# A new written order of the neighbourhood layer's parts in a period, and of the recurrence's units between them

## The chip, the cores and the metric

The kernel runs on one core of one Trainium2 chip. The metric is the device time of one execution in microseconds; of the kernel before there are three timed runs. The profile is of one further execution.

## The reference

Input `x` is (4, 56, 56, 128): four images of 3136 tokens with 128 channels. Four layers follow one another, each with residual sums. The change concerns the first two:

```python
# layer 0: 7x7 neighbourhood attention with 4 heads, then an MLP (128 -> 512 -> 128)
x = x + proj(softmax(q . k over the 7x7 window + rpb) @ v)      # q, k, v from layernorm(x)
x = x + gelu(layernorm(x) @ w_fc1 + b_fc1) @ w_fc2 + b_fc2
# layer 1: group norm, then 16 steps of a gated complex recurrence per position and channel
x = x + recurrence(gn(x))
#   forget = sigmoid(x Wf + bf + 2); let_in = sigmoid(x Wi + bi); delta = softplus(x Wd + bd) * 0.1
#   h <- forget * (A h) + delta * let_in * (B x), with A and B from 7x7 kernels by a Fourier transform
```

Layers 2 and 3 are softmax attention, mixtures of experts, a distance attention and expert choice. They come later in the program and their code is the same in both kernels.

## The kernel before

`neighbourhood_of_safe_scores` (L471) works layer 0 off in 28 stripes: 4 images times 7 stripes of 8 image rows, 448 tokens each. A stripe passes through 25 parts, small functions that each issue a few instructions: two of attention scores (`scores`, `more_scores`: TensorE at L653, the exponential on ScalarE at L662), the position bias (`bands`, `more_bands`: VectorE, L669), the sums over neighbours and their denominators (`start_sums`, `sums`, `more_sums`: TensorE, L683 to L711), `quotient` (VectorE, L719 and L720), `project` and `add_attention` (L725 to L737), `second_norm` (VectorE, L739: statistics, then an inverse root of twelve small steps that ends with `off`, L546), `norm_mlp` and `mlp_tokens`, `mlp_hidden` (TensorE L754, GELU on ScalarE L759), `mlp_out` (L768) and `add_mlp` (L778). `norm_ahead`, `tokens`, `keys` and `queries` prepare a stripe three ahead (L583 to L618), `values` makes v (L635 and L639), `statistics` takes the first norm's statistics of stripes further on, up to three of them a period, until all are taken.

The parts are written out in the table `PERIOD` as (name, lag): in period i the part works on stripe i + lag. The loop of L867 runs i from -1 to 29. Everything in it stands in a manual schedule (L827): TensorE, VectorE and ScalarE issue their instructions in exactly this written order, each in its own queue, and wait for one another by semaphores only. So the table's order is the order of each of the three queues.

Between the parts lies the recurrence of image 0, at places which three more tables give as (period after the start, position in the period, name): a piece at position p is issued just ahead of the p-th part.

```python
for i in range(-1, n + 2):
    for at, (name, lag) in enumerate(PERIOD):
        run_all(plan.get((i, at), ()))
        if 0 <= i + lag < n:
            parts[name](i + lag)
    run_all(plan.get((i, len(PERIOD)), ()))
```

`WAVES_AT` places the eight transform steps that make A and B (L1033 to L1072), one starting in each of the periods 1 to 8. `BEGIN` places the group norm of image 0 from period 8 on: `tokens` (28 transposes and seven ScalarE sums, L1095), `mean`, `squares` (seven ScalarE passes, L1112), `root`, `normalise`. `WORK` places the pieces of each of seven units (a quarter of the rows of `parts`, L1128), the first from period 10 and one every two periods. A unit has three gates on TensorE and ScalarE (`delta`, `forget`, `let_in`: L1159 and L1164), copies (`turned`, L1181), a logarithm (L1188), and some forty VectorE instructions over 224 or 448 columns (L1185 to L1282). Even periods from 10 to 24 are called even below; in the kernel before, most of a unit's VectorE work lies in an even period.

[...] Scores and the MLP's hidden sums share one buffer of four banks, the sums have two, and all else on TensorE shares a pool of two banks (`ps1`): `mlp_out`, `values` (two tiles), both token transposes, `keys`, `queries`, `project`, the gates, the transform's products and `turned_back`. A tile that takes one of these banks waits for the reader of an earlier tile.

ScalarE's functions need tables. `exp_table` and `gelu_table` (L825) call the function on one column, so that the table is loaded there. The functions of the recurrence (sigmoid, logarithm, square root) load others.

Of the kernel before, what the change touches and what calls it, by code (L numbers as in the profile page):

```python
# [38 lines left out]
NQ = EC // ET  # L39

PERIOD = (
    ("mlp_out", -2),
    ("exp_table", 1),
    ("norm_mlp", -1),
    ("more_sums", 0),
    ("norm_ahead", 3),
    ("scores", 1),
    ("add_mlp", -2),
    ("values", 1),
    ("more_scores", 1),  # L50
    ("tokens", 3),
    ("mlp_tokens", -1),
    ("quotient", 0),
    ("keys", 3),
    ("bands", 1),
    ("constants", 1),
    ("queries", 3),
    ("project", 0),
    ("start_sums", 1),
    ("more_bands", 1),  # L60
    ("add_attention", 0),
    ("mlp_hidden", -1),
    ("gelu_table", -1),
    ("second_norm", 0),
    ("sums", 1),
    ("statistics", 1),
)

WORK = (
    (0, 20, "delta"),  # L70
    (0, 23, "turned"),
    (1, 12, "softplus"),
    (1, 12, "sources"),
    (1, 14, "logarithm"),
    (1, 18, "let_in"),
    (1, 19, "forget"),
    (1, 21, "softplus_sum"),
    (1, 22, "source"),
    (1, 24, "source_gate"),
    (2, 4, "traces"),  # L80
    (2, 4, "fourths"),
    (2, 5, "fourths_trace"),
    (2, 7, "sums"),
    (2, 7, "sums_of_fourths"),
    (2, 11, "product_of_sums"),
    (2, 14, "pair"),
    (2, 18, "steps"),
    (2, 20, "result"),
    (2, 21, "result_sum"),
    (3, 1, "turned_back"),  # L90
    (3, 2, "added"),
    (4, 25, "statistics"),
)

BEGIN = (
    (0, 25, "tokens"),
    (1, 11, "mean"),
    (1, 14, "squares"),
    (1, 22, "root"),
    (2, 12, "normalise"),  # L100
)

WAVES_AT = (
    (0, 11, "products"),
    (1, 17, "squared"),
    (1, 17, "magnitudes"),
    (2, 10, "scaled"),
)
UNITS = 9
KK = 128  # L110
# [360 lines left out]
def neighbourhood_of_safe_scores(env: Env, f, work):  # L471
# [17 lines left out]
    with ExitStack() as ctx:  # L489
# [337 lines left out]
        with tc.manual_schedule(  # L827
# [39 lines left out]
# [7 lines that stand above are left out]
# [1839 lines left out]
def run_all(pieces):  # L2713
    for piece in pieces:
        piece()
# [201 lines left out]
```

## Time and profile before

| | |
|---|---|
| median of three runs | 2683.82 us (2681.54 to 2685.61) |
| the profiled execution's own time | 2683.05 us |
| its span, first to last instruction | 2681.3 us |
| TensorE, VectorE, ScalarE busy | 2484.3, 2025.0, 1688.4 us |
| start of the first scores (L653) / end of the last `add_mlp` (L778), where the next layer begins | 32.85 us / 690.9 us |

The stage that the tables order is thus the stretch from 32.85 to 690.9 us, a quarter of the span. A busy TensorE is not TensorE at its peak, since the ends of matmuls are modelled. Idle time is listed before an instruction, with what ended it; on an engine that doesn't set the pace it costs nothing.

### The profile page before, as it was taken

What the parts mean: (1) busy time and instruction counts of PE and PEld (TensorE: products, weight loads), DVE (VectorE), ACT (ScalarE), POOL (GpSimd) and SP (SyncE); (2) the same over time, 40 slices, a digit from 0 to 9 for tenths busy, and PEclk for the clock granted to TensorE, in tenths of its full rate; (3) what the DMA queues carried; (4) which work ended last, traced back from release to release, by engine and by line L of the source; (5) the groups of instructions that cost most, each with busy time, mean ns of one, the idle gap of its engine ahead of it and who ended that gap; (6) DMA issues with size and microseconds to landing.
All of it is one profiled execution on the core that took longest, in us unless ns stands there. A gap on an engine that the chain in (4) does not pass through costs nothing.

```text
span 2681.3 us, 40144 instructions
## 1 busy us (share of the span) xinstructions
PE 2484.3 (93%) x14849; PEld 1338.1 (50%) x14849; DVE 2025.0 (76%) x5777; ACT 1688.4 (63%) x3539; POOL 4.4 (0%) x34
## 2 busy tenths in 40 slices
PE   5998898889999999999999999999999998997795
PEld 4676666667544544444454444444444443442333
DVE  6877999998488785879958877863788676766564
ACT  3789777775578774767733366565555565753671
POOL 0000000000000000000000000000000000000000
PEclk8999999999999999999999999999999998997687
DMA  5000000000000000000000000000000000001265
GB/s 134 10 10 2 2 2 2 2 1 2 9 1 1 1 0 1 1 1 1 0 11 0 1 1 1 1 1 1 1 1 1 0 1 1 1 1 75 98 251 180
DMA packets 39924, 54.01 MB, mean 20 GB/s; under 512 B 4105, under 2 KB 35444, under 8 KB 35621
## 3 DMA queue, kind: packets, MB, share of 16 engines
q1 hardware_dynamic: 39716, 51.34, 6.0%
q8 instruction: 119, 1.95, 0.3%
q14 instruction: 89, 0.72, 0.1%
HBM read 44.78 MB, written 6.42 MB: 19 GB/s over the span
## 4 chain that ended last, share of the span: by engine, by line


## 5 line engine op out<-in xcount | busy, mean ns | idle before, releaser
L1969 PE MATMUL s_ps<-zT,xnT 128*128 128x448 f32 (+1 forms) x1400 | 652.9, 557 | 11.6 <-ACT e L1976 11.2
L2052 PE MATMUL o_ps<-e,keep 128*128 128x448 f32 (+1 forms) x1376 | 645.6, 553 | 0.0
L1976 ACT ACTIVATE e<-s_ps 128x448 f32<-128x448 f32 x688 | 363.9, 542 | 444.3 <-PE s_ps L1969 436.4
L1969 PEld LDWEIGHTS s_ps<-zT,xnT 128*128 128x128 f32 (+1 forms) x1400 | 238.1, 189 | 232.4 <-issue 181.5
L2052 PEld LDWEIGHTS o_ps<-e,keep 128*128 128x128 f32 (+1 forms) x1376 | 242.0, 190 | 218.1 <-issue 216.9
L1783 ACT ACTIVATE d_ps<-d_ps,half 112x448 f32<-112x448 f32 x412 | 249.2, 606 | 157.5 <-PE d_ps L1772 156.3
L1777 DVE TENSOR_REDUCE found<-d_ps 112x1 f32<-112x448 f32 x372 | 224.3, 618 | 74.5 <-PE d_ps L1772 71.1
L1513 PE MATMUL y_ps<-experts,xnT 128*112 128x512 f32 x448 | 217.8, 608 | 3.4 <-ACT d_ps L1783 2.4
L1518 DVE TENSOR_TENSOR gated<-y_ps,gate 112x512 f32<-112x512 f32 x224 | 151.6, 687 | 47.2 <-PE y_ps L1513 45.1
L1772 PE MATMUL d_ps<-q_near,k_near 32*112 32x448 bf16 x784 | 154.6, 410 | 14.9 <-ACT d_ps L1783 7.7
L1523 DVE TENSOR_TENSOR gated<-gated 112x512 f32<-112x512 f32 (+1 forms) x336 | 152.7, 462 | 3.3
L202 PE MATMUL xT_ps<-ident,xn 112*128 112x112 f32 x672 | 112.4, 280 | 28.6 <-ACT xn L1613 18.6
L1772 PEld LDWEIGHTS <-k_near 32*112 32x112 bf16 x784 | 47.0, 126 | 178.6 <-issue 166.7
L202 PEld LDWEIGHTS xT_ps<-ident,xn 112*128 112x128 f32 x672 | 79.1, 145 | 99.1 <-ACT xn L1613 54.5
L1513 PEld LDWEIGHTS y_ps<-experts,xnT 128*112 128x112 f32 x448 | 75.8, 179 | 99.8 <-issue 60.1
L768 PE MATMUL f_ps<-w_fc,h 128*112 128x128 f32 x896 | 113.1, 282 | 4.7 <-ACT h L759 3.9
L1613 ACT ACTIVATE xn<-x,g_off,g_rs 112x128 f32<-112x128 f32 x224 | 94.5, 484 | 26.2 <-DVE g_off L1603 9.7
L768 PEld LDWEIGHTS f_ps<-w_fc,h 128*112 128x112 f32 x896 | 102.8, 179 | 15.5 <-ACT h L759 10.0
L583 ACT ACTIVATE xn<-x,off,rs 112x128 f32<-112x128 f32 x224 | 89.3, 480 | 30.3 <-DVE off L546 30.3
L669 DVE TENSOR_TENSOR e<-e,band 112x1792 f32<-112x1792 f32 (+3 forms) x56 | 98.9, 1783 | 4.4 <-ACT e L662 4.4
L754 PE MATMUL h_ps<-zT,w_fc 128*128 128x448 f32 x224 | 101.4, 600 | 0.6 <-ACT zT L748 0.6
L1164 ACT ACTIVATE parts<-g_ps,gates_b 128x224 f32<-128x224 f32 x168 | 65.6, 445 | 57.6 <-PE g_ps L1159 45.0
(387 smaller groups left out, 4057.9 us busy)
## 6 DMA issues: line engine op xcount, KB each, us to landing
lot<-in_L_ffn_lots SPq DMA_DIRECT2D x32, 1024.0 KB
out_x<-x SPq DMA_DIRECT2D x28, 224.0 KB
x<-in_x SPq DMA_DIRECT2D x3, 1568.0 KB
x<-in_x SPq DMA_DIRECT2D x7, 224.0 KB
parts<-in_waves SPq DMA_DIRECT2D x8, 173.0 KB
out<-found SPq DMA_DIRECT2D x64, 2.0 KB
w_fc<-in_L_conv_w_fc SPq DMA_DIRECT2D x2, 256.0 KB
experts<-in_L_ffn_expert_w SPq DMA_DIRECT2D x1, 512.0 KB
```

Source lines behind the costliest of these rows:

```text
L202: self.nc.tensor.transpose(ps[:, j * P : (j + 1) * P], xn[:, j, :], self.ident[:P, :P])
L754: nc.tensor.matmul(h_ps[:, k, :GW], w_fc1[:, k * 128 : (k + 1) * 128], held[i]["zT"], start=True, stop=True,)
L768: nc.tensor.matmul(f_ps[:, j, :], h[:, k, j * P : (j + 1) * P], w_fc2[:, k, :], start=(k == 0), stop=(k == 3),)
L1513: nc.tensor.matmul(y_ps, held["xnT"][g][:, j * P : (j + 1) * P], self.experts[:, 4 * i : 4 * i + 4, :], start=True, stop=True,)
L1518: nc.vector.tensor_tensor(gated[:, some, :], y_ps, gate[:, some].unsqueeze(2).to_broadcast([P, 4, C]), ALU.mult,)
L1523: nc.vector.tensor_tensor(gated[:, :n, :], gated[:, :n, :], gated[:, n : 2 * n, :], ALU.add)
L1772: nc.tensor.matmul(d, held["k"][part, h, :], held["q"][g][part, :], start=True, stop=True)
L1777: nc.vector.tensor_reduce(self.found[:, self.most : self.most + 1], d, AX.X, ALU.max)
L1783: nc.scalar.activation(d, d, AF.Relu, bias=self.half, accum_out=self.found[:, self.sums : self.sums + 1],)
L1969: nc.tensor.matmul(s_ps[i * n : (i + 1) * n, :GW], self.xnT[:, at : at + n], zT, start=True, stop=True,)
L1976: nc.scalar.activation(e[:n], s_ps[:n, :GW], AF.Exp)
L2052: nc.tensor.matmul(sums[:, :GW], self.keep[:n, k, :], e[:n], start=(k == 0 and g - 1 not in pairs), stop=last,)
```

## The change

Four tables get other contents. No part, no instruction and no size is changed. In `PERIOD` all 25 entries stand as before with the same lags, in another order: `more_sums` comes ahead of `mlp_out`; `mlp_tokens` ahead of the scores; `statistics` moves from the end to behind `more_scores`; `add_mlp` moves behind `values` and `statistics`; `project` and `start_sums` move ahead of `keys`, and `queries` to the end; `sums` moves ahead of `add_attention`; `gelu_table` moves ahead of `mlp_hidden`; `more_bands` moves behind `sums`.

The units begin three positions later (`delta` at position 23). `softplus_sum`, `source` and `source_gate` move from the end of the odd period to the start of the even one, the gates `let_in` and `forget` to position 22, behind the GELU. `sums_of_fourths` to `steps` stand together at position 13, ahead of `bands`. The group norm's `mean` and `squares` move to the start of period 9, and `normalise` to position 22 of period 10.

```diff
 PERIOD = (
+    ("more_sums", 0),
+    ("norm_mlp", -1),
+    ("exp_table", 1),
     ("mlp_out", -2),
-    ("exp_table", 1),
-    ("norm_mlp", -1),
-    ("more_sums", 0),
     ("norm_ahead", 3),
+    ("mlp_tokens", -1),
     ("scores", 1),
-    ("add_mlp", -2),
     ("values", 1),
     ("more_scores", 1),
+    ("statistics", 1),
+    ("add_mlp", -2),
     ("tokens", 3),
-    ("mlp_tokens", -1),
     ("quotient", 0),
-    ("keys", 3),
+    ("constants", 1),
     ("bands", 1),
-    ("constants", 1),
-    ("queries", 3),
+    ("gelu_table", -1),
     ("project", 0),
     ("start_sums", 1),
+    ("keys", 3),
+    ("mlp_hidden", -1),
+    ("sums", 1),
+    ("add_attention", 0),
+    ("queries", 3),
     ("more_bands", 1),
-    ("add_attention", 0),
-    ("mlp_hidden", -1),
-    ("gelu_table", -1),
     ("second_norm", 0),
-    ("sums", 1),
-    ("statistics", 1),
 )
 
 WORK = (
-    (0, 20, "delta"),
     (0, 23, "turned"),
-    (1, 12, "softplus"),
-    (1, 12, "sources"),
-    (1, 14, "logarithm"),
-    (1, 18, "let_in"),
-    (1, 19, "forget"),
-    (1, 21, "softplus_sum"),
-    (1, 22, "source"),
-    (1, 24, "source_gate"),
-    (2, 4, "traces"),
-    (2, 4, "fourths"),
-    (2, 5, "fourths_trace"),
-    (2, 7, "sums"),
-    (2, 7, "sums_of_fourths"),
-    (2, 11, "product_of_sums"),
-    (2, 14, "pair"),
-    (2, 18, "steps"),
-    (2, 20, "result"),
-    (2, 21, "result_sum"),
-    (3, 1, "turned_back"),
-    (3, 2, "added"),
+    (0, 23, "delta"),
+    (1, 4, "softplus"),
+    (1, 13, "logarithm"),
+    (1, 14, "sources"),
+    (1, 22, "let_in"),
+    (1, 22, "forget"),
+    (2, 1, "softplus_sum"),
+    (2, 2, "source"),
+    (2, 2, "source_gate"),
+    (2, 7, "traces"),
+    (2, 7, "fourths"),
+    (2, 8, "fourths_trace"),
+    (2, 10, "sums"),
+    (2, 13, "sums_of_fourths"),
+    (2, 13, "product_of_sums"),
+    (2, 13, "pair"),
+    (2, 13, "steps"),
+    (2, 21, "result"),
+    (2, 22, "result_sum"),
+    (3, 3, "turned_back"),
+    (3, 8, "added"),
     (4, 25, "statistics"),
 )
 
 BEGIN = (
-    (0, 25, "tokens"),
-    (1, 11, "mean"),
-    (1, 14, "squares"),
-    (1, 22, "root"),
-    (2, 12, "normalise"),
+    (0, 23, "tokens"),
+    (1, 0, "mean"),
+    (1, 5, "squares"),
+    (2, 2, "root"),
+    (2, 22, "normalise"),
 )
 
 WAVES_AT = (
-    (0, 11, "products"),
-    (1, 17, "squared"),
-    (1, 17, "magnitudes"),
-    (2, 10, "scaled"),
+    (0, 9, "products"),
+    (1, 12, "squared"),
+    (1, 12, "magnitudes"),
+    (2, 1, "scaled"),
 )
```

## The prediction

> **What bounds the kernel now.** I read the page first, then busy time by stages, then the timeline and the table of waits inside the stages. The page says only that TensorE is busiest overall:
>
> ```profile
> span 2681.3 us, 40144 instructions
> PE 2484.3 (93%) x14849; PEld 1338.1 (50%) x14849; DVE 2025.0 (76%) x5777; ACT 1688.4 (63%) x3539; POOL 4.4 (0%) x34
> ```
>
> The four tables order only 32.85 to 690.9 us, so I cut that stretch where its limits change (the columns are us, then busy time of PE, PEld, DVE, ACT, POOL, then the granted clock):
>
> ```profile
> 32.85:95.99 63.14, 52.84 (x679) 40.24 (x679) 51.26 (x195) 33.13 (x62) 0.00 (x0) 0.81 0.29 62
> 95.99:221.62 125.63, 119.69 (x1598) 90.79 (x1594) 102.25 (x270) 113.42 (x194) 0.00 (x0) 1.00 0.03 9
> 221.62:310.51 88.89, 78.48 (x964) 58.79 (x964) 71.23 (x188) 76.68 (x140) 0.00 (x0) 0.98 0.01 2
> 359.36:409.10 49.74, 45.22 (x558) 33.66 (x557) 46.95 (x118) 36.98 (x65) 0.00 (x0) 0.90 0.01 2
> 554.22:601.70 47.48, 42.07 (x540) 31.09 (x536) 44.04 (x102) 36.73 (x65) 0.00 (x0) 0.96 0.01 2
> 630.33:690.90 60.57, 53.88 (x634) 40.48 (x632) 39.23 (x111) 29.00 (x52) 0.48 (x9) 0.97 0.00 1
> ```
>
> Row 2 is six periods of pure PE work: 95% busy. Rows 4 and 5 are two pairs of periods with a recurrence unit in each: DVE 94%, and the rest is mostly the step from one instruction to the next. So there are five pieces: a head, a PE-bound piece, the group norm's start, the DVE-bound units (310.51 to 630.33), a tail. In the PE-bound piece the timeline shows one real gap per period, and in the units the other things that matter, a wait for `quotient` and half-speed matmuls after it (L683 takes 1.86 us instead of 1.02):
>
> ```profile
> 183.10 0.98 PE L202 MATMUL xT_ps<-ident,xn 112*128 112x112 f32 x8
> 184.99 1.55 PE L1043 MATMUL f_ps<-parts,taps 113*64 113x196 f32 x16 [0.91 <-ACT xnT L599]
> 189.39 1.02 PE L683 MATMUL d_ps<-outside,pad_w 49*128 49x448 f32 x2
> ...
> 326.96 1.17 PE L730 MATMUL y_ps<-w_proj,oT 128*112 128x128 f32 x8 [2.42 <-DVE oT L720]
> 328.05 1.86 PE L683 MATMUL d_ps<-outside,pad_w 49*128 49x448 f32 x2
> ```
>
> [...] The trace shows such stretches in multiples of 3.41 us, but in the units after gaps of 2.3 to 2.5 us already (four of the five PE waits of that size), so I use the trace. [...]
>
> **The change, part by part.** Durations are steps from one start to the next in the timeline. No instruction and no DMA is added. The only DMAs in moved parts are the eight of `in_waves`; SP keeps their order, and their buffers come free earlier. Nothing is queued on POOL. Table loads: four per period in the PE-bound piece (exp, square root, sigmoid, GELU) and six per pair of unit periods, both before and after: `delta` behind the GELU loads exp itself, and the next `exp_table` then finds it there.
>
> *Head.* `statistics` now stands ahead of the first `bands` and the late constants on DVE. It fills DVE waits of 4.37, 2.88 and 0.37 us, but three stripes (4.17 us each) hold `bands` from 36.8 to 48.7 us, and `sums` on PE with it. The second scores then start at 56.6 instead of 52.4 us. DVE owes less afterwards (7.4 us); by the fourth scores I get 95.5 instead of 95.99. Gain 0.5.
>
> *PE-bound periods.* PE's parts add up to 19.75 us (20.4 with an edge stripe). The gap of 0.91 between `tokens` and what follows goes: `project` and `start_sums` (2.2 us) now cover ScalarE's copy. In its place `tokens` waits 0.32 us for a `ps1` bank, since the transform's copies come behind the second exponential (1.2 us). With 0.07 at `more_scores` that makes 20.2 instead of 20.73; ScalarE (18.9) and DVE (18.2 to 20.0) fit below. Six periods: gain 3.0.
>
> *Group norm's start.* `tokens` costs ScalarE 4.8 us, `squares` 5.4. New: `squares` stands ahead of the copy of zT and the exponential in period 9, so PE waits 3 us for a bank and runs at half speed for about 6.8 us (3 us lost). `delta` of unit 0 waits for `normalise` and `queries`, and DVE idles 4.4 us before `softplus`. Adding up from the scores of period 8 to the end of `second_norm` of period 11: 85.7 us against 88.9 (where DVE waited 7.8 us for `mlp_out` and 4.3 for `mean`). But then 1.8 us of DVE work (`softplus_sum`, `source`) that was done by then is still to do. Gain 1.4.
>
> *Units.* DVE's work per pair: twice 12.3 (`second_norm` 4.2, `quotient` 3.5, bands 3.4, two sums 1.2) and 21.2 for the unit, 45.9; with `statistics` (1.6 a period, until period 17) 49.0. Measured pairs were 48.9, 49.7, 51.9 (an inverse root of 2.65 in it), 45.9, 47.4, 47.5: waits of 4.6 us in six and a half pairs. That is all the units can give. In the new order DVE has 30.5 us of work in an even period and 15.4 in an odd one (each plus 1.6), so in the odd ones a chain must keep up. From the end of `second_norm` (off, L546): norms 0.15 to 3.45 (eight of 0.385 and steps between), copy of zT to 3.9, exponential to 5.6, `more_scores` 6.45, `tokens` 6.95, `project` behind `quotient` to 8.75, `start_sums` 9.8, `keys` 10.65, `mlp_hidden` 13.85, four GELUs 16.1, table 17.4, `let_in` 18.2. DVE needs it for `source_gate` after 0.78 + 0.54 + 0.65 + 1.6 + 0.6 + 3.5 + 1.1 + 1.9 + 0.6 + 1.5 + 4.2 + 1.9 = 18.9: margin 0.7. Without `statistics` it needs it at 17.3 and has it at 17.5: wait 0.2 to 0.35, and 0.65 more before an edge stripe. Ahead of the chain, `turned` and `delta` (with a table load, 5.4 us behind `result_sum`) end 0.3 us before `second_norm` does. In even periods PE waits 2.4 us at `values` (`add_mlp` now lies behind 7.9 us of unit work and `statistics`), 1.4 at `project` and up to 2.0 for `more_bands`; the first two cost nothing while DVE is busy, the last stands at the head of the chain: if PE is then at half speed, `mlp_out` ends 2.4 us later. I take 0.2 us a pair for four pairs, 1.7 for the last three together, and 0.7 for half speed: 3.2 in place of 4.6. Gain 1.4.
>
> *Tail.* Without units, `mlp_out` behind `more_sums` and ahead of `add_mlp`, then `quotient`, delays `quotient` by 0.9 us in period 26, of which 0.8 reaches the end. Loss 0.8.
>
> Sum: 0.5 + 3.0 + 1.4 + 1.4 - 0.8 = 5.5 us. The profiled execution took 2683.05 us, 1.75 more than its span, and 0.8 less than the median; its span would become 2675.8, and the median 2683.8 - 5.5 = 2678.3. What follows at 690.9 us is unchanged.
>
> Bounds of what the trace doesn't show: the head -2 to +7 (DVE's whole idle time), half-speed stretches in the start 0 to 3 us (shown by L683's 1.86 against 1.02), and in the units 0 to 2 us a pair.
>
> **Rivals.** *Larger gain.* The head keeps its 7.2 us of filled DVE idle time, because PE's later start is made up by fewer waits in the next two periods, and the odd chain never holds DVE: 7.2 + 3.0 + 1.4 + 4.6 - 0.8 = 15.4 at most, about 11 if half of the head's gain is eaten: 2673. For it: DVE has no gap from 45 to 95 us. Against it: PE has to restart at 56.6 us at half speed.
>
> *Slower.* The odd chain decides. If every wait for `more_bands` is followed by a half-speed stretch (four of five long waits were), the chain starts 2.4 us late, and DVE waits 1.7 us where the margin is 0.7 and about 2.5 where it is none: with the edge 0.65, 4 x 1.7 + 3 x 2.5 + 0.65 = 15. The other terms give 0.5 + 3.0 + 1.4 + 4.6 - 0.8 = 8.7, so the change loses from 8.7 / 7 = 1.2 us a pair on; at 15 it loses 6: 2690. Against it: in the even periods the earlier waits take the half-speed stretch first, where it is hidden, and then PE comes late enough to have less than 1 us left to wait.
>
> *No change.* DVE's work is fixed and bounds 310 to 630 us, and the start of the units is delayed by as much as PE gained before: 2683.
>
> **How the numbers follow.** Within 0.2% (5.4 us) is about what a measurement of this kernel can't tell from no change. Forecast 0.48 (own range 2673 to 2683; 0.30 of it faster, 0.18 same), larger gain 0.22, no change 0.10, slower 0.20. Faster: 0.30 + 0.22 = 0.52; same 0.18 + 0.10 = 0.28; slower 0.20. The range runs from the larger gain, with the head's bound partly taken, to the slower case: 2669 to 2690.
>
> **What would show it.** Right: periods of 20.2 us at full clock in the PE-bound piece, with no wait on xnT L599; `bands` at about 48.7 us; pairs of 46 to 49 us in the units, DVE idle before `source_gate` (L1198) below 1 us; `values` waiting for add_mlp in even periods. Wrong: DVE idle of over 1.2 us a pair before L1198, L778 or L1185 in the units; half-speed `mlp_out` at the head of odd periods; a PE-bound period still at 20.7; a tail more than 2 us longer; or any change behind the stage's end.

## The result and the profile after

The change makes the kernel slightly faster: the median goes from 2682.26 us (ten runs, 2679.13 to 2687.31) to 2673.87 us (ten runs, 2668.07 to 2679.25), a ratio of 0.9964 with a 95% interval of 0.9954 to 0.9975. 2678.3 had been forecast, in a range of 2669 to 2690. The profiled execution of the changed kernel took 2678.24 us against 2683.05, so it is one of its slower ones; the last section comes back to that spread.

The page of the changed kernel, its lines for the span and the busy time: the engines have the same work, and the span is 4.9 us shorter.

```profile
span 2676.4 us, 40173 instructions
PE 2478.0 (93%) x14849; PEld 1336.8 (50%) x14849; DVE 2024.6 (76%) x5777; ACT 1690.3 (63%) x3539; POOL 4.3 (0%) x34
```

Busy time by stages, cut at the same events as before (us, then busy PE, PEld, DVE, ACT, POOL, granted clock): the head, the six PE-bound periods, the group norm's start, two pairs of unit periods, the tail.

```profile
32.71:94.51 61.80, 51.11 (x684) 37.31 (x684) 56.10 (x223) 33.44 (x62) 0.00 (x0) 0.83 0.31 67
94.51:215.00 120.49, 118.19 (x1596) 90.01 (x1595) 100.82 (x253) 112.80 (x193) 0.00 (x0) 1.00 0.03 9
215.00:298.41 83.41, 77.24 (x979) 59.28 (x980) 66.65 (x181) 74.36 (x137) 0.00 (x0) 0.96 0.01 2
349.43:398.60 49.17, 42.06 (x542) 32.03 (x538) 46.92 (x117) 37.82 (x65) 0.00 (x0) 0.97 0.01 2
544.45:591.36 46.91, 41.18 (x534) 31.78 (x530) 44.06 (x102) 37.19 (x65) 0.00 (x0) 0.96 0.01 2
621.93:685.86 63.93, 56.63 (x609) 43.10 (x607) 39.05 (x111) 31.07 (x54) 0.48 (x9) 0.93 0.00 1
```

Against the rows of before, the head is 1.3 us shorter, the PE-bound piece 5.1, the start 5.5. In the PE-bound piece TensorE's idle time fell from 5.94 us (125.63 - 119.69) to 2.30, and its busy time by 1.5. The units as a whole (298.41 to 621.93) are 3.7 us longer, the tail 3.4 longer: 4.9 us are left. What follows took 1990.3 us before and 1990.6 after, to the end of the span.

The timeline of TensorE in one PE-bound period of the changed kernel shows what the gap became: the transform's matmuls (L1043) now come first, `tokens` waits 0.31 us for a bank, and `keys` (L605) finds its operand ready.

```profile
137.88 1.55 PE L1043 MATMUL f_ps<-parts,taps 113*64 113x196 f32 x16
139.74 0.60 PE L202 MATMUL xT_ps<-ident,xn 112*128 112x112 f32 x4 [0.31 <-ACT fa L1047]
140.18 0.38 PE L725 MATMUL y_ps<-proj_parts,pick 96*112 96x512 bf16 x1
...
142.36 1.02 PE L605 MATMUL k_ps<-xnT,w_qkv 128*128 128x448 f32 x2
```

In the units VectorE sets the pace (busy for 302.6 of 323.5 us), so its waits are the loss. The table of VectorE's waits from 298.41 to 621.93 us of the changed kernel (waiter, what it waited for, us in total, times, longest):

```profile
DVE parts L1185 <- ACT parts L1175: 3.6, 2, 2.1
DVE x L778 <- PE f_ps L768: 1.9, 2, 1.0
DVE parts L1198 <- ACT parts L1164: 1.7, 3, 0.7
```

and the same table of the kernel before, from 310.51 to 630.33 us:

```profile
DVE x L737 <- PE y_ps L730: 3.0, 2, 1.5
DVE x L1298 <- PE y_ps L1291: 1.1, 2, 0.6
```

7.2 us of waiting took the place of 4.1; VectorE's busy time is 302.6 against 301.9. These 3.1 + 0.6 are the 3.7. The waits are others than before: for `delta` (L1185 is `softplus`), `mlp_out` and `let_in` instead of `project` and `turned_back`.

### The profile page after: what moved, and what is told of

Its sections match the earlier page's. It is cut to its first block, busy times and chain, and to the rows that moved or that the text cites. A ratio compares the mean times of both kernels' runs of the same rounds, so it can differ in the third digit from the quotient of the medians.

```text
span 2676.4 us, 40173 instructions
## 1 busy us (share of the span) xinstructions
PE 2478.0 (93%) x14849; PEld 1336.8 (50%) x14849; DVE 2024.6 (76%) x5777; ACT 1690.3 (63%) x3539; POOL 4.3 (0%) x34
## 4 chain that ended last, share of the span: by engine, by line
## 5 line engine op out<-in xcount | busy, mean ns | idle before, releaser
L1969 PE MATMUL s_ps<-zT,xnT 128*128 128x448 f32 (+1 forms) x1400 | 654.3, 559 | 11.6 <-ACT e L1976 11.2
L1969 PEld LDWEIGHTS s_ps<-zT,xnT 128*128 128x128 f32 (+1 forms) x1400 | 238.5, 189 | 232.3 <-issue 181.5
L1613 ACT ACTIVATE xn<-x,g_off,g_rs 112x128 f32<-112x128 f32 x224 | 94.5, 484 | 26.2 <-DVE g_off L1603 9.7
L669 DVE TENSOR_TENSOR e<-e,band 112x1792 f32<-112x1792 f32 (+3 forms) x56 | 99.8, 1784 | 0.0
L759 ACT ACTIVATE h<-h_ps,b_fc 128x448 f32<-128x448 f32 x112 | 61.9, 635 | 55.3 <-PE h_ps L754 55.3
L754 PE MATMUL h_ps<-zT,w_fc 128*128 128x448 f32 x224 | 94.9, 569 | 0.6 <-ACT zT L748 0.6
```

Of the source, the lines that this page charges most:

```text
L669: nc.vector.tensor_tensor(es, es, bands[stripes[i][1] == 0][:n].rearrange("p h r c -> p h (r c)").unsqueeze(2) .to_broadcast([n, NH, m, 8 ...
L1969: nc.tensor.matmul(s_ps[i * n : (i + 1) * n, :GW], self.xnT[:, at : at + n], zT, start=True, stop=True,)
```

## The experiments

Every kernel below moves entries of the written order and nothing else. The diffs show the list entries; the positions of the units are renumbered so that a unit keeps its neighbours. The table gives the stages from one profile each, in us, and the ratio to the kernel before, which was timed anew beside each group of runs. A stage in which nothing was changed differed by up to 0.9 us in the head, 0.1 in the PE-bound piece, and 1.9 in the tail (K3's against the changed kernel's), so smaller differences there say nothing. The start is equal to 0.1 us in pairs that differ in `more_bands` alone (the changed kernel and K4, K3 and K8). For the units there is no such pair, so there a difference is read together with the waits behind it.

| | head | PE-bound | start | units | tail | ratio (95%) |
|---|---|---|---|---|---|---|
| before | 63.1 | 125.6 | 88.9 | 319.8 | 60.6 | |
| changed | 61.8 | 120.5 | 83.4 | 323.5 | 63.9 | 0.9964 (0.9954 to 0.9975) |
| K1 | 66.8 | 127.4 | 103.7 | 349.5 | 64.5 | 1.0192 (1.0177 to 1.0207) |
| K2 | 63.2 | 126.5 | 94.4 | 328.5 | 62.0 | 1.0045 (1.0029 to 1.0060) |
| K3 | 61.0 | 120.5 | 81.6 | 324.5 | 62.1 | 0.9961 (0.9945 to 0.9977) |
| K4 | 61.1 | 120.5 | 83.4 | 319.6 | 62.3 | 0.9956 (0.9942 to 0.9971) |
| K5 | 63.5 | 124.8 | 88.3 | 322.9 | 63.5 | 1.0031 (1.0020 to 1.0042) |
| K6 | 60.9 | 120.3 | 85.7 | 328.2 | 61.9 | 0.9985 (0.9975 to 0.9995) |
| K7 | 64.0 | 122.3 | 87.4 | 323.0 | 62.8 | 0.9985 (0.9977 to 0.9993) |
| K8 | 61.8 | 120.5 | 81.6 | 320.3 | 62.2 | 0.9951 (0.9936 to 0.9966) |
| K9 | 61.8 | 128.0 | 85.0 | 325.8 | 62.4 | 1.0007 (0.9998 to 1.0017) |
| K10 | 61.9 | 123.1 | 96.6 | 338.9 | 62.8 | 1.0084 (1.0069 to 1.0098) |
| K11 | 61.0 | 120.5 | 86.9 | 390.4 | 62.9 | 1.0240 (1.0224 to 1.0256) |
| K12 | 61.6 | 120.4 | 96.7 | 339.0 | 62.8 | 1.0083 (1.0066 to 1.0099) |

### The gap of 0.91 us: K1, K2, K5, K10, K12

**K1**, the kernel before with the two readers of xnT behind `project` and `start_sums`:

```diff
-    ("keys", 3),
     ("bands", 1),
     ("constants", 1),
-    ("queries", 3),
     ("project", 0),
     ("start_sums", 1),
+    ("keys", 3),
+    ("queries", 3),
```

> The kernel before, with keys and queries moved behind project and start_sums, nothing else. My theory (the gap on xnT is the whole of what the change removes in the PE-bound piece): the wait of 0.91 us on xnT L599 goes, the period of that piece falls from 20.73 to about 19.8 us, six periods give 5 to 5.5 us, the units keep their lengths (the gap lay beside VectorE there), and the whole comes to about 2677 us. Rival (the gap only moves: project then waits for oT of quotient, L720->L730): the period stays at 20.5 us or more and the whole within 1 us of before.

Both theories missed. The period rose to 21.37 us, and the gap neither went nor moved to oT: TensorE's timeline of K1 shows the same 0.91 us ahead of matmuls that don't read xnT at all.

```profile
168.01 0.98 PE L202 MATMUL xT_ps<-ident,xn 112*128 112x112 f32 x8
169.91 1.55 PE L1043 MATMUL f_ps<-parts,taps 113*64 113x196 f32 x16 [0.91 <-ACT xnT L599]
```

So it is a wait for a bank. `ps1` has two; `tokens` takes one, `mlp_tokens` directly behind it the other, and the third tile needs the first bank back, which ScalarE's copy of xnT frees. That was to be read in the trace of before too: there L1043 had the same 0.91. (The other loss of K1, in the units, comes below with K12.)

**K2**, the changed kernel with `keys` back behind `tokens`:

```diff
     ("tokens", 3),
+    ("keys", 3),
     ("quotient", 0),
...
     ("start_sums", 1),
-    ("keys", 3),
```

> The changed kernel with keys put back directly behind tokens, nothing else. My theory: the wait on xnT L599 is back with 0.9 us beside the bank wait of 0.3, the period of the PE-bound piece goes from 19.87 to about 20.8 us, and the piece is 5 us longer, so the whole is near 2679 us. Rival (the shorter matmul streams, 0.26 us a period, and the other places of mlp_out and mlp_tokens make the shorter period): keys finds its tokens copied, the period stays below 20.2 us, the whole near 2674 us.

The theory held: a period of 20.87 us, the PE-bound piece 6.0 longer. Here it is the operand that is waited for; the timeline of K2 has both waits:

```profile
164.15 0.60 PE L202 MATMUL xT_ps<-ident,xn 112*128 112x112 f32 x4 [0.30 <-ACT fa L1047]
165.47 1.02 PE L605 MATMUL k_ps<-xnT,w_qkv 128*128 128x448 f32 x2 [0.72 <-ACT xnT L599]
```

The whole lost 22 us to the changed kernel, most of it (11.0 and 5.0) in the start and the units.

**K5**, the kernel before with the two transpositions set apart:

```diff
     ("norm_ahead", 3),
+    ("mlp_tokens", -1),
     ("scores", 1),
...
     ("tokens", 3),
-    ("mlp_tokens", -1),
```

> The kernel before, with mlp_tokens moved from behind tokens to ahead of scores, nothing else; keys and queries stay where they were. My theory now (the 0.91 us is a wait for a bank: two ps1 banks, tokens takes one, mlp_tokens the other, and the third user waits until ScalarE has copied xnT out of the first): with a scores and a values part between the two transpositions the 0.91 us goes, the period of the PE-bound piece falls from 20.73 to 19.8 us (six periods 5.5), and in the units nothing or up to 1 us a pair, whole 2675 to 2679 us. Rival (keys needs its own operand xnT, so that its place alone decides): the period stays at 20.5 us or more, whole 2683.

The period only fell to 20.60, which meets the rival's number but not its reason. `tokens` was now followed by the transform's two groups, each with a bank, and it was the second one that waited; in K5's timeline:

```profile
161.50 0.60 PE L202 MATMUL xT_ps<-ident,xn 112*128 112x112 f32 x4
162.03 0.88 PE L1043 MATMUL f_ps<-parts,taps 113*64 113x196 f32 x8
163.40 0.88 PE L1043 MATMUL f_ps<-parts,taps 113*64 113x196 f32 x8 [0.48 <-ACT xnT L599]
```

**K10**, the kernel before with K5's move and two more:

```diff
-    ("keys", 3),
     ("bands", 1),
     ("constants", 1),
-    ("queries", 3),
     ("project", 0),
     ("start_sums", 1),
+    ("keys", 3),
...
     ("sums", 1),
+    ("queries", 3),
     ("statistics", 1),
```

> The kernel before, with three moves together: mlp_tokens ahead of scores, keys behind start_sums, queries behind sums. Each of the first two kinds alone left a wait of 0.5 to 0.9 us and did not shorten the period (21.37 and 20.60 against 20.73). Theory (three users hang on the one copy of xnT: the bank through mlp_tokens, the operand through keys, and the y_ps bank through queries, so the gap goes only when all stand away from it): no wait on xnT L599 and none on x L737, the period of the PE-bound piece 19.8 to 20.2 us, the piece 3 to 5 us shorter than 125.6. Rival (something else in the new order, mlp_out behind more_sums or tokens behind the transform's matmuls, makes the short period): 20.5 us or more. The units may go either way here, and the whole with them.

20.30 us: the 0.48 was still there, as the place of the transform's products had been left alone; the theory was incomplete. **K12** moves them too, from behind `tokens` to ahead of it, with `mlp_out` still ahead of `more_sums` and `statistics` still last:

```diff
 WAVES_AT = (
-    (0, 11, "products"),
+    (0, 10, "products"),
```

> The three moves on the kernel before (mlp_tokens ahead of scores, keys behind start_sums, queries behind sums; period 20.30 us, with 0.48 us left at the transform's second group of matmuls, which waits for the bank that xnT is copied out of), and a fourth: the transform's products ahead of tokens. Theory (two banks, and every user two places behind tokens waits for ScalarE's copy): the 0.48 us goes, 0.31 us of wait for the copy of fa L1047 ahead of tokens takes its place, and the period is 19.9 us as in the changed kernel, with mlp_out still ahead of more_sums; the piece is 120 to 121.5 us. Rival (mlp_out behind more_sums, or statistics, has a part in the 19.87): 20.1 us or more. The units stay as long as with three moves, the whole near 2702 us.

19.84 us, and 120.35 for the piece: the whole gain of the PE-bound periods from these four moves. The timeline of K12 reads like that of the changed kernel:

```profile
137.76 1.55 PE L1043 MATMUL f_ps<-parts,taps 113*64 113x196 f32 x16
139.61 0.60 PE L202 MATMUL xT_ps<-ident,xn 112*128 112x112 f32 x4 [0.31 <-ACT fa L1047]
140.05 0.38 PE L725 MATMUL y_ps<-proj_parts,pick 96*112 96x512 bf16 x1
```

Yet K12 as a whole is 0.8% slower than before, as it loses 19 us in the units and 8 in the start. In the units its tables of waits, VectorE's and TensorE's, have one long line each:

```profile
DVE x L1298 <- PE y_ps L1291: 23.1, 5, 5.7
```

```profile
PE y_ps L730 <- DVE oT L720: 30.8, 7, 4.7
```

In an even period TensorE comes to `project` before VectorE has ended `quotient`, and stands waiting for oT (4.4 us each time; 13.0 in all in the kernel before, 8.9 in the changed one). `keys` now stands behind that wait, and `queries` too, ahead of `mlp_out`; the gate `delta` and `mlp_hidden` stood behind it before as well. The work behind the wait is also slower, as in this period of K12:

```profile
534.63 2.05 PE L730 MATMUL y_ps<-w_proj,oT 128*112 128x128 f32 x8 [3.65 <-DVE oT L720]
536.61 1.86 PE L683 MATMUL d_ps<-outside,pad_w 49*128 49x448 f32 x2
539.89 1.86 PE L605 MATMUL k_ps<-xnT,w_qkv 128*128 128x448 f32 x2
```

The two later groups take 1.02 us at a granted clock of 1.00 (L683 at 189.4 us in the kernel before, L605 at 142.4 in the changed one); the kernel before shows the 1.86 us of L683 in a stretch with a granted clock of 0.50 (327.9 to 334.7 us). K12's four timed runs have a mean granted clock of 0.945 to 0.950, those of the kernel before beside them 0.957 to 0.960. So `mlp_out` and `turned_back` come late, and VectorE waits for that at the head of the odd period. How the 19 us divide between the longer queue and the half clock isn't shown. The moves that free TensorE in the PE-bound periods thus cost the units dear where `quotient` comes late.

### Is it the period or the units' places: K11

**K11** has the changed `PERIOD`, with the units beside VectorE's parts about where they stood before:

```diff
-    (0, 23, "turned"),
-    (0, 23, "delta"),
-    (1, 4, "softplus"),
...
-    (2, 13, "sums_of_fourths"),
-    (2, 13, "product_of_sums"),
-    (2, 13, "pair"),
-    (2, 13, "steps"),
-    (2, 21, "result"),
+    (0, 19, "delta"),
+    (0, 20, "turned"),
+    (1, 13, "softplus"),
...
+    (2, 11, "sums_of_fourths"),
+    (2, 12, "product_of_sums"),
+    (2, 15, "pair"),
+    (2, 21, "steps"),
+    (2, 22, "result"),
```

> The changed order of the neighbourhood layer's parts, with the recurrence's units put back to about where they stood before beside VectorE's parts: softplus and sources behind quotient, pair behind bands, result behind add_attention, softplus_sum and source_gate at the end of the odd period, gates ahead of mlp_hidden; normalise behind quotient. Theory (the period's order brought the gains and the units' new places cost the 3.7 us of the units): head 61.8 and PE-bound piece 120.5 as in the changed kernel, units 316 to 320, start 82 to 86. Rival (the units' new places are what makes the new period work: in the odd periods VectorE has little to do while TensorE catches up): units 325 or more, TensorE late for mlp_out L778 or y_ps L1298, whole 2676 or more.

Head and PE-bound piece are those of the changed kernel, as both theories had it: they belong to the period's order. In the units the kernel can't be used as it stands. With `turned` ahead of `result`, the next unit's copies overwrite `pq`, so `result` computes with other values than the recurrence's and also waits for the copies. That is the first of the lines of VectorE's waits in K11's units:

```profile
DVE parts L1274 <- ACT parts L1181: 63.5, 6, 11.6
DVE x L778 <- PE f_ps L768: 11.4, 5, 3.0
```

Without the 63.5 us (and 1.0 at L1278) the units would be 326 us by subtraction. TensorE waited 30.8 us for oT, as in K12, and in period 24, where no next unit copies anything, still 4.44. That speaks for the rival: `sums_of_fourths` and `product_of_sums` stand ahead of `quotient` here, as in the kernel before, and behind it in the changed kernel, where the wait for oT is about 1.1 us in most even periods. A clean run of the old places was not made, so the size stays open.

### The units and the start: K3, K4, K8

**K3**, `softplus` away from the wait for `delta`:

```diff
-    (1, 4, "softplus"),
     (1, 13, "logarithm"),
+    (1, 14, "softplus"),
     (1, 14, "sources"),
```

> The changed kernel with the unit's softplus moved on VectorE from the head of the odd period to ahead of sources, so that delta has time to end. My theory (the units lost 3.7 us because VectorE waits for delta at softplus L1185, 4.22 + 2.09 + 1.48 us): these waits go, source_gate L1198 waits at most 1 us more, and the stretch from the second_norm of period 11 to that of period 24 is 2 to 4 us shorter, with 2 to 4 more off the start of unit 0; whole near 2668 us. Rival (VectorE is only let off to wait for the next thing, add_mlp or y_ps, because TensorE is late itself after half-speed stretches): the stretches change by less than 1 us, whole near 2674 us.

The rival holds in the units. VectorE's waits in K3's units:

```profile
DVE x L778 <- PE f_ps L768: 4.8, 4, 1.4
DVE parts L1198 <- ACT parts L1164: 3.3, 4, 1.2
```

No wait for `delta` is left, and the sum is 8.1 us instead of 7.2: VectorE was let off one late result to wait for the next. TensorE's chain was late. Only the start, where `delta` itself was last, gained 1.8 us.

**K4**, `more_bands` directly behind `bands`:

```diff
     ("bands", 1),
+    ("more_bands", 1),
     ("gelu_table", -1),
...
     ("queries", 3),
-    ("more_bands", 1),
     ("second_norm", 0),
```

> The changed kernel with more_bands moved from the end of the period to directly behind bands. My theory (in the even periods TensorE waits 1.4 to 3.9 us for more_bands, then starts the odd period late and partly at half speed): the wait DVE e L669->L705 goes, the tail (end of second_norm 24 to the last add_mlp) is 2.5 to 3 us shorter, the units 1 to 3 us shorter, whole near 2669 us. Rival (the wait is hidden beside VectorE, which bounds the units; more_bands only trades places with result and add_attention, and project's bank or the second norm come later): units unchanged or up to 2 us longer, tail at most 1 us shorter, whole within 1.5 us of 2674.

The late `more_bands` was the cause of the units' loss. Busy time of K4 in the units and in the tail:

```profile
297.88:617.46 319.58, 279.61 (x3505) 206.87 (x3501) 302.80 (x720) 239.37 (x414) 0.00 (x0) 0.95 0.01 2
617.46:679.78 62.32, 52.83 (x579) 39.31 (x579) 39.25 (x111) 30.96 (x54) 0.48 (x9) 0.95 0.01 1
```

The units are 3.9 us shorter than in the changed kernel and as long as before; TensorE's wait for e L669 fell from 13.6 to 2.5 us, VectorE's waits from 7.2 to 2.8 us, and the granted clock of the units rose from 0.94 to 0.95. K8 below, which has the same move, agrees (320.3 us), and K3, which lacks it, stays at 324.5. The timed runs don't separate K4 from the changed kernel: the intervals of their ratios overlap.

**K8**, both moves:

```diff
     ("bands", 1),
+    ("more_bands", 1),
...
-    ("more_bands", 1),
...
-    (1, 4, "softplus"),
+    (1, 14, "softplus"),
```

> The changed kernel with more_bands directly behind bands and softplus ahead of sources. More_bands alone took 3.9 us off the units and 1.6 off the tail, softplus alone 1.8 off the start of the group norm and nothing off the units, where VectorE then waited for mlp_out and let_in instead. Theory (TensorE's chain decides, and more_bands early sets it ahead, so that the softplus move now counts): VectorE's waits in the units fall from 2.8 to about 1 us, the start is 1.8 us shorter, whole about 2669 us. Rival (the two do not add): units within 1 us of 319.6, start within 0.5 us of 83.6, whole near 2672.

They nearly add: start 81.6, units 320.3 (0.7 more than K4), and VectorE's waits 3.5 us, not the 1 expected. The stage is 6.8 us shorter than in the changed kernel; the ratio of 0.9951 is the best of all, though its interval overlaps that of the changed kernel.

### The tail, the head and what didn't help: K6, K7, K9

**K6**, `mlp_out` back ahead of `more_sums`:

```diff
+    ("mlp_out", -2),
     ("more_sums", 0),
     ("norm_mlp", -1),
     ("exp_table", 1),
-    ("mlp_out", -2),
```

> The changed kernel with mlp_out put back ahead of more_sums at the head of the period, nothing else. The step of the prediction on the tail (mlp_out behind more_sums and ahead of add_mlp, then quotient, costs the last periods 0.8 us): the tail is 1 to 2.5 us shorter. It also lets VectorE wait less for f_ps L768->L778 at the end, and in the units the odd chain gains up to 1.3 us. Rival (the tail is longer because more_bands is late at the end of period 24, not because of mlp_out's place): the tail stays within 0.5 us of 63.8, and quotient, now waiting for more_sums behind mlp_out, makes the units up to 1 us a pair longer. Whole 2671 to 2673 by the first, 2674 to 2680 by the second.

The tail is 2.0 us shorter, no more than K3's tail was without any change of its own, so it decides nothing. The units are 4.7 us longer, as VectorE waits more:

```profile
DVE parts L1185 <- ACT parts L1175: 5.7, 3, 2.7
DVE parts L1198 <- ACT parts L1164: 4.8, 5, 1.8
```

The new place of `mlp_out` is therefore good for the units.

**K7**, `statistics` back at the end of the period:

```diff
     ("more_scores", 1),
-    ("statistics", 1),
     ("add_mlp", -2),
...
     ("second_norm", 0),
+    ("statistics", 1),
```

> The changed kernel with statistics put back to the end of the period, nothing else. By the prediction's step on the head (VectorE's filled idle time is eaten by the later bands, net gain 0.5 us): the head, from the first scores to those of the fourth stripe, stays within 1 us of 61.8, and the start of the second scores moves from 57.6 to 52 to 54 us. Rival (the filled idle time is kept, up to 7.2 us): the head is 3 to 7 us longer. PE-bound periods stay at 19.9 us in both. Whole within 2 us of 2674 by the first, 2677 to 2681 by the second.

The second scores start at 51.3 us instead of 57.6, and still the head is 2.2 us longer, the PE-bound piece 1.8 (in one period TensorE waits 1.65 us for `add_mlp`), the start 4.0. The rival is nearer: the filled idle time of VectorE is partly kept, and pays in three stages. In the start, VectorE's waits in K7 are other and more than the changed kernel's, with 2.2 for the exponential and 3.2 for `project`:

```profile
DVE mean L1092 <- PE g_ps L1090: 5.6, 1, 5.6
DVE parts L1185 <- ACT parts L1175: 4.3, 1, 4.3
DVE x L737 <- PE y_ps L730: 3.2, 2, 2.1
DVE x L778 <- PE f_ps L768: 2.2, 2, 1.2
DVE e L669 <- ACT e L662: 2.2, 1, 2.2
```

**K9**, K8 with two more moves:

```diff
-    (1, 0, "mean"),
+    (1, 1, "mean"),
...
+    ("add_mlp", -2),
     ("statistics", 1),
-    ("add_mlp", -2),
```

> The kernel with more_bands early and softplus late (start 81.8, units 320.3, tail 62.0), and two more moves: the group norm's mean behind the first transform's last part instead of ahead of more_sums, so that VectorE does 2.8 us of that part while ScalarE copies the tokens; and add_mlp ahead of statistics, so that values gets its bank earlier. Theory (TensorE's 2.6 us wait for add_mlp in the start, and up to 2.3 in even periods, come from what stands ahead of add_mlp on VectorE): the first wait falls below 0.5 us, VectorE's wait for mean from 8.2 to 5 to 6.5 us, the start is 2 to 3 us shorter, units and tail within 1.5 us. Rival (ScalarE bounds that period with 28.4 of 29.4 us): the start is at most 1 us shorter.

It lost everything K8 had gained. VectorE's waits from 94.6 to 123.1 us, at the start of the PE-bound piece:

```profile
DVE x L778 <- PE f_ps L768: 11.2, 2, 6.0
```

`add_mlp` ahead of `statistics` takes from VectorE the work that filled the wait for `mlp_out`: one period is 7.5 us longer, the start 3.4, the units 5.6. The wait for `mean` did fall, to 3.6, but 3.2 us for `mlp_out` came behind it.

## Why the prediction was right, point by point

The sum of 5.5 us stands against 4.9 in the profiles and 8.4 in the medians. The range of 2669 to 2690 holds the median, but the parts were off by more than the sum.

- **PE-bound periods: predicted 3.0, measured 5.1.** The wait in front of `tokens` (0.32 predicted, 0.31 found) and the 0.07 at `more_scores` were right, and no wait for xnT was left. Those three terms add up to 20.14 us, which the prediction rounded up to 20.2; unrounded, six periods give 3.5, and the idle time did fall by 3.6. Mis-sized was TensorE's own part, taken as an unchanged 19.75 us: it is 19.49, with `mlp_out` at 3.75 us instead of 3.87, for example. The reason given, that `project` and `start_sums` cover the copy, is half of it: K1 puts them in between and keeps the gap. The new places of `mlp_tokens`, `keys`, `queries` and the transform's products together are enough (K12). Without the products 0.48 us stays (K10), and with `keys` early the wait is back (K2); whether `queries` had to move wasn't tried alone.
- **Head: predicted 0.5, measured 1.3.** The step was right on the later second scores (56.6 against 57.6) and on the small net gain; the start of the fourth was put at 95.5 and came at 94.5. K7 shows that `statistics` also helps the two pieces behind the head, 1.8 and 4.0 us, which the step didn't have.
- **Group norm's start: predicted 3.2 less 1.8 of work still owed, measured 5.5.** The idle time ahead of `softplus` was right (4.4 against 4.22). The 3 us to be lost at half speed were mis-sized: TensorE waited 2.64 us, not for the bank of zT but at `values` for `add_mlp`, and one stretch of 3.4 us at half clock followed (a granted clock of 0.50 from 245.0 to 248.4 us), not 6.8 (a second one stands 41 us later). At half the clock these 3.4 us lose some 1.7, an estimate from the two figures, so this explains 1.3 of the 2.3 us between 3.2 and 5.5; the rest is open.
- **Units: predicted waits of 3.2 us, measured 7.2 (4.1 before).** This step failed. It let `turned` and `delta` end 0.3 us ahead of `second_norm`, which left no wait; VectorE waited for `delta` 2.1 and 1.5 us. The mechanism was the one of the slower rival: `more_bands` late at the end of the even period (13.6 us of waits on TensorE), TensorE late in the odd one. It reached about half of that rival's size. K4 takes it away and with it all of the loss; K3 shows that `delta` was only the first to show it.
- **Tail: predicted a loss of 0.8 from `mlp_out` in period 26, measured 3.4.** The step named the wrong place. From `second_norm` 25 to 27 the kernel took 31.9 us against 31.8, and K6, with `mlp_out` back in its old place, 31.6. Of the loss 2.6 lies in period 25, 16.44 us against 13.86, and 0.6 behind the last `second_norm`. In the changed kernel's timeline TensorE waits there for `more_bands`, and `mlp_out` behind it takes 5.00 us, against 3.75 in the PE-bound piece; the granted clock is 0.50 from 617.0 to 623.9 us:

```profile
617.97 0.60 PE L705 MATMUL o_ps<-e,v 112*32 112x112 f32 x8 [2.77 <-DVE e L669]
...
621.11 5.00 PE L768 MATMUL f_ps<-w_fc,h 128*112 128x128 f32 x32
```

With `more_bands` early period 25 takes 13.95 (K4); with it late, 15.2 to 15.3 in K2, K3 and K7. Those three have tails of 62.0 to 62.8, so 1 to 2 us of the 3.4 may be chance.
- **Behind the stage:** unchanged in the two profiles, as predicted. The medians moved by 3.5 us more than the spans. That would fit runs in which this part takes some 6 us less, as it does in other profiles (last section); nine of the changed kernel's ten runs have no trace, so it isn't shown.

So the time was right by luck: two gains larger than predicted (5.1 and 5.5) met a loss in the units, where a gain had been forecast, and a loss in the tail larger than predicted. The median of 2673.87 even lies nearer to the 2673 of the rival with the larger gain than to 2678.3, yet that rival's mechanism isn't what the profile shows: the odd periods did hold VectorE. Of the prediction's signs of being right, `bands` came at 48.6 us, `values` waited for `add_mlp`, and no wait for xnT was left; of its signs of being wrong, the tail more than 2 us longer and `mlp_out` at half speed at the head of an odd period (the 5.00 us above) came too.

## What to carry over

A wait that the timeline puts down to a copy was here one for data (0.72 us in K2) or for the buffer which the copy empties (0.91 in K1, 0.48 in K5); whether the waiting instruction reads what was copied tells which, and with two buffers every tile two places behind was a candidate, so one move alone did not free it. In an order written by hand, a part that the next engine needs at the turn of the period (here `more_bands`) belongs ahead of work that nobody waits for, even if the engine that does both is busy without a gap; and independent work (here `statistics`) belongs in front of a wait, not behind it. The kernel with the shortest stage here is K8, the change with `more_bands` behind `bands` and `softplus` behind `quotient`; in the whole time the runs don't separate it from the changed kernel, K3 and K4.

## What the runs showed of the hardware

The part behind the stage is the same code in all fourteen kernels, yet in their profiles it took 1976.2 to 1977.0 us in seven and 1967.2 to 1973.8 in six (K11, whose recurrence computes other values, left out), from the last `add_mlp` to the end of the last engine instruction. The kernel before (1976.2 us) and the changed one (1976.8) are among the longer. Each has a stretch of 3.41 us at a granted clock of 0.50 that begins 2.2 us (before) or 2.9 us (changed) behind the last `add_mlp`, and a second one 330 us behind it. The waits ahead of the first are 1.20 us, then 0.79 (before) or 0.73 (changed). The changed kernel, in TensorE's timeline:

```profile
686.26 0.99 PE L202 MATMUL xT_ps<-ident,xn 112*128 112x112 f32 x4 [1.20 <-DVE xn L1910]
687.99 0.55 PE L1924 MATMUL keep_ps<-ident,xnT 128*128 128x128 f32 x3 [0.73 <-DVE xnT L176]
688.37 1.36 PE L1945 MATMUL z_ps<-xnT,z_w 128*128 128x448 f32 x2
```

and K4, one of the shorter, with the same two waits:

```profile
680.19 1.00 PE L202 MATMUL xT_ps<-ident,xn 112*128 112x112 f32 x4 [1.20 <-DVE xn L1910]
681.91 0.55 PE L1924 MATMUL keep_ps<-ident,xnT 128*128 128x128 f32 x3 [0.73 <-DVE xnT L176]
682.29 0.92 PE L1945 MATMUL z_ps<-xnT,z_w 128*128 128x448 f32 x2
```

The two matmuls of L1945 take 1.36 us in the changed kernel and 0.92 in K4, the two of L1969 behind them 1.80 us (at 690.50) and 1.02 (at 684.04).

In the trace of the kernel before there are 24 stretches at a granted clock of 0.50, in that of the changed one 25. Each begins a whole multiple of 3.4133 us behind the beginning of the one before it, to 0.01 us. What decides whether such a stretch follows a gap was not shown.

The timed runs spread with their clocks: of the ten of the changed kernel, the five above 2675 us have a mean granted clock of 0.954 to 0.957, the five below 2673 us one of 0.959 to 0.962.

For a stage of 650 us in a kernel of 2680 this matters: landmarks inside a profile tell 1 us, while ten runs of one kernel spread over 8 to 11. Gaps of 1.20 and 0.73 us with 1 us of matmul between them were followed by a half-speed stretch in one of the two profiles shown and not in the other.
